# Products of rotated weights half a key step later, transposed results copied in halves, convolution rows loaded piece by piece

## The chip, the cores and the metric

The kernel runs on one core of a Trainium2 chip. The metric is the device time of one execution in microseconds (us), the median of the runs shown. In the profile, PE is TensorE (PEld its weight loads), DVE is VectorE, ACT is ScalarE, POOL is GpSimd, and SP is SyncE, whose queue issues all DMA transfers of this kernel.

## The reference, cut to what matters

Sixteen images of 256 channels and 64 x 64 pixels go through two layers, each of the form `x = x + f(groupnorm(x))`. Layer 0 is a grouped 3 x 3 convolution whose weights are rotated for each image by an angle that depends on the image. Layer 1 is linear attention with a 5 x 5 depthwise convolution of the values.

```python
# layer 0, f = rotated group convolution
pooled = x.mean(axis=(2, 3))
h = relu(pooled @ ap_w1.T + ap_b1)
angles = tanh(h @ ap_w2.T + ap_b2) * (pi / 4)
rot = vmap(vmap(_rotate_one))(base_kernel, angles)   # bilinear: 9 x 9 mixing of each 3 x 3 kernel
out = conv(x, rot, groups=B * G, padding=1)
feat = out * sigmoid(relu(pooled @ meta_w1.T + meta_b1) @ meta_w2.T + meta_b2)
# layer 1, f = focused linear attention
q = focus(relu(xt @ Wq.T + bq)); k = focus(relu(xt @ Wkv_k.T + bk)); v = xt @ Wkv_v.T + bv
z = 1 / (q . k.sum() + 1e-6)                          # focus: r -> r**3 * |r| / |r**3|
out = (q @ (k.T @ v)) * z + depthwise5x5(v) + dwc_b
out = out @ Wproj.T + bproj
```

All arithmetic is in float32.

## The kernel before

Everything is one hand-written order of instructions for each engine (`tc.manual_schedule()`, main loop from L930). An engine runs its instructions in the order in which the program emits them, so a place in this order is a place in every queue. The images overlap: while image b is in its attention, image b+1 is convolved, and image b+2's statistics are taken.

One image b of the main loop has three parts.

**Key steps** (`key_step`, L774). Sixteen steps n, of which images 1 to 15 do the first three already at the end of the previous image's attention, so that their loop starts at n = 3 (`LEAD`). Step n makes the keys and values of 256 pixels on PE (`key_products`, L559, two halves j), and adds bias and applies relu on DVE (`key_bias`: L528, L529, and L568 for the values). The focus function of a key block is spread over later steps: squares of block n-1 on ACT (L535), its cube on POOL (L538), then one step later the ratio on DVE (L543, L544), the root on POOL (L547) and the scaling on ACT (`key_scale`, L579). `values` (L592) multiplies scaled keys with values on PE into `pkv`: block 0 at step 3, then at each odd step blocks n-4 and n-3. `key_store` (L573, SP) writes the values to a DRAM image `vpad`, and `load_blocks` (L614, SP) reads them back as `vh`, the blocks of the depthwise convolution, two transfers a step from step 7 to step 14.

Beside the key steps runs the preparation of image b+1's rotated weights, a Python generator `prepare` (L190) called `made` in the loop. Each `next(made)` emits the instructions up to the next `yield`; `key_step` calls it twice a step, in the middle (after the first half's bias) and at the end. For image 0's key steps, `made` starts at step 1. For later images it starts with three advances in the attention steps p = 15, 16 and 17 of the image before, and goes on at step 3. The generator makes the angle terms, then for each half t of the channels and each n three kernel rows: `products` (L285, POOL, 128 x 864 elements), a pause, `reduce` (L301, DVE), a pause. After the third one `finish` adds row sums on DVE (L305) and the identity on POOL (L311). `spread` (L316, ACT) copies the result into the weight tile `wt`, and `shifts` (L324 to L328) makes the edge corrections in the last advance.

**Between** (`between`, L800). PE computes the first query block (L654), convolution unit 0 of image b+1 (L406, 288 products on 32 x 32 tiles), the remaining `values`, and the first half of the depthwise products `pd` (L629, 256 matmuls).

**Attention steps** (`attention_step`, L839), p = 1 to 17. Step p turns queries (`turn`, L669; copy `turned`, L674), multiplies them with the key-value state (`attend`, L686, result `o` on POOL, L697), turns the result of block p-2 back (`turn_back`, PE L705, copied from PSUM to the tile `oT` by ACT, L707) and projects it (`project`, L715). `project` has four products, two per half t of `oT`, in the order t = 0, 1, 0, 1. `add_up` (L727) and `store` (L733) finish block p-3; the store is one transfer for two blocks. Convolution units 1, 2 and 3 of image b+1 are emitted at the end of steps 3, 7 and 11 (`UNITS`), their evictions (L419) in the step after. The second depthwise half stands in step 9. Image b+2's statistics are loaded (L97) and taken (L106) in steps 3, 5, 7, 9 and 11 (`STATS`); there is one buffer for them, so a load waits on SP until DVE has taken the one before.

A convolution unit reads four pieces of rows, one per quarter q of the partitions (`xr`, one buffer for all images after image 0). `load_rows` (L376, SP) issues the four transfers of a unit together: unit 0 at key step 11, unit 1 in `between` ahead of the depthwise products, units 2 and 3 in attention steps 4 and 8, ahead of the stores. `load_edges` (L390, POOL) fills the rows beyond the image in the first and last pieces.

Of the kernel before, what the change touches and what calls it, by code (L numbers as in the profile page):

```python
# [15 lines left out]
P = 128  # L16
C = 256
H = W = 64
N = H * W
HID = 64  # L20
NH, HD = 8, 32
CH = 512
NCH = N // CH
# [5 lines left out]


UNITS, SECOND = {3: 1, 7: 2, 11: 3}, 9

STATS = {3: (0, 1), 5: (2,), 7: (3, 4), 9: (5, 6), 11: (7,)}
CROWS = CH + 2 * W
# [16 lines left out]
def conv_attention(ctx: ExitStack, tc: tile.TileContext, x, consts, kw, b1, w2, b2, b2r,  # L51
                   wkv, wq, brow, srow, wp, bp, dwb, band, out):
    nc = tc.nc
# [30 lines left out]
    state = {}  # L84
# [59 lines left out]
    def rows_of(b, u):  # L144
        return xbuf[u if b == 0 else 0]
# [44 lines left out]
    def prepare(b):  # L190

        a, pooled, mean = yield from gn_coefs(state[b]["st"], b, 0)
# [36 lines left out]
        edge = wtp.tile([P, NH], F32, tag="edge", name=f"edge_{b}")  # L229
# [2 lines left out]
        nc.vector.tensor_copy(edge, pe)  # L232
        state[b]["edge"] = edge
        if b == 0:
            load_edges(0, 0)
        nc.vector.tensor_scalar(mod, mod, 0.5, 0.5, ALU.mult, ALU.add)
        yield

# [93 lines left out]
        if b == 0:  # L332
            made = {k: products(*k) for k in ((0, 0), (0, 1), (0, 2), (1, 1), (1, 2))}
            made[1, 0] = own_products(1, 0)
            for t in range(2):
                for n in range(3):
                    reduce(t, n, made[t, n])
                row_sums(t)
                nc.vector.scalar_tensor_tensor(rots[t][:, 4], sel[:, 0:HD], 1.0, rots[t][:, 4], ALU.mult, ALU.add)
                if t == 0:  # L340
                    spread(0, range(4))
            for j in range(3):
                for q in (1, 3):
                    nc.vector.tensor_copy(wt[ts(q, HD), j], rots[1][ts(j, HD)])
            spread(1, (3,))
            state[b]["late"] = shifts
            return
        for t in range(2):
            for n in range(3):
                tmp = products(t, n)  # L350
                if t == 1 and n < 2:
                    spread(0, (2 * n,))
                yield
                reduce(t, n, tmp)
                if n == 2:
                    finish(t)
                yield
                if t == 1 and n < 2:
                    spread(0, (2 * n + 1,))
        for j in range(4):  # L360
            spread(1, (j,))
            yield
        for _ in range(3):
            yield
        shifts(0)
        shifts(1)

    def load_rows(b, u):


        for q in range(4):
            i, t = 2 * u + q // 2, q % 2
            lo, hi = max(0, CH * i - W), min(N, CH * (i + 1) + W)
            d = rows_of(b, u)[ts(q, HD)]
            at = W if i == 0 else 0
            nc.sync.dma_start(d[:, :, at:at + hi - lo], x[b, ts(t, P)].rearrange("(g c) n -> c g n", g=4)[:, :, lo:hi])  # L376

    def load_edges(b, u):


        for q in range(4):
            i, t = 2 * u + q // 2, q % 2
            mean = state[b]["edge"][ts(q, HD), ts(t, 4)].unsqueeze(2).to_broadcast([HD, 4, W])
            d = rows_of(b, u)[ts(q, HD)]
            for edge, at in ((0, 0), (NCH - 1, CROWS - W)):
                if i == edge:
                    if b == 0:
                        nc.scalar.copy(d[:, :, at:at + W], mean)
                    else:
                        nc.gpsimd.tensor_copy(d[:, :, at:at + W], mean)  # L390

    def convolve(b, u):

# [48 lines left out]
    nc.gpsimd.tensor_scalar(su, se, 1.0, None, ALU.add)  # L442
    nc.scalar.activation(sa, su, AF.Ln)
    for u in range(NCH // 2):
        load_rows(0, u)
    for i in range(2):
        load_stats(1, i)
    eps_t = const("eps", [P, C])
# [3 lines left out]
    for name, src, bsrc in (("kv", wkv, brow[C:3 * C]), ("q", wq, brow[0:C])):  # L452
        n = src.shape[1]
# [29 lines left out]
    for (w, br), lo in zip(wl.values(), (0, 2 * C)):  # L483
# [3 lines left out]
        n = w.shape[2]  # L487
# [82 lines left out]
    def key_store(b, n):  # L570
        for j in range(2):
            k, y = (2 * n + j) % BC, ROWS * (n // 2) + 2
            nc.sync.dma_start(vpad[b % 2][k, y:y + ROWS].rearrange("y j n -> (y j) n"),  # L573
                              vbuf[n % NV][:, j, 0:HD, :].rearrange("p c h -> p (c h)"))
# [125 lines left out]
    def turn_back(b, m):  # L700

        po = bank(f"po_{b}_{m}").rearrange("p (t j n) -> p t j n", t=2, j=2)
        for j in range(2):
            for t in range(2):
                nc.tensor.transpose(po[:, t, j, :], state[b]["o"][j][:, ts(t, P)], ident)  # L705
        oT = op.tile([P, 2, 2 * P], F32, tag="oT", name=f"oT_{b}_{m}", bufs=1)
        nc.scalar.copy(oT.rearrange("p t (j n) -> p t j n", j=2), po)  # L707
        state[b]["oT"] = oT

    def project(b, m):  # L710
# [29 lines left out]
    for u in range(NCH // 2):  # L740
        convolve(0, u)
        if u == 0:
            for t in range(2):
                state[0]["late"](t)
            load_edges(0, NCH // 2 - 1)
            for i in range(2, 6):
                load_stats(1, i)
        else:
            for i in {1: (0, 1), 2: (2, 3), 3: (4, 5)}[u]:
                take_stats(1, i)  # L750
                if u == 2:
                    load_stats(1, i + 4)
        for q in range(4):
            evict(0, u, q)
            settle(0, u, q)
# [44 lines left out]
    def between(b, more):  # L800

        k, f = state[b]["k"], state[b]["f"]
        query_products(b, 0)
        if more:
            convolve(b + 1, 0)
        ratio(k[NP - 2], False)
        root(k[NP - 2])
        squares(k[NP - 1], 0)
        cube(k[NP - 1])
        key_scale(b, NP - 2)  # L810
        query_bias(b, 0)
        blocked(b, 2)
        squares(k[NP - 1], 1)
        ratio(k[NP - 1], False)
        root(k[NP - 1])
        key_scale(b, NP - 1)
        squares(f[0], 0)
        cube(f[0])
        for n in range(NP - LATE, NP - 1):
            values(b, n)  # L820
        query_products(b, 1)
        query_bias(b, 1)
        values(b, NP - 1)
        if more:
            for q in range(4):
                evict(b + 1, 0, q)
        squares(f[0], 1)
        squares(f[1], 0)
        if more and b + 2 < B:
            load_stats(b + 2, 0)  # L830
        if more:
            load_rows(b + 1, 1)
        for c in range(0, HD, 4):
            depthwise(b, 0, c)
        if more:
            for q in range(4):
                settle(b + 1, 0, q)

    def attention_step(b, p, chain):  # L839
# [3 lines left out]
        more = b + 1 < B  # L843
# [69 lines left out]
        if p <= NCH:  # L913
            load_blocks(b, 2 * p + 14)
            load_blocks(b, 2 * p + 15)
        if u and u < 3:
            load_edges(b + 1, u + 1)
            load_rows(b + 1, u + 1)
        if p >= 3:
            store(b, p - 3)  # L920
        if n >= 1:
            key_store(b + 1, n - 1)
        if more and p in UNITS:
            u = UNITS[p]
            convolve(b + 1, u)
# [4 lines left out]
    with tc.manual_schedule():  # L930
        fold_load(0, "q")
        made = iter(())
        for b in range(B):
            more = b + 1 < B
            state[b]["f"], state[b]["xq"] = {}, {}
            for n in range(0 if b == 0 else LEAD, NP):
                if b == 0 and n == 0:
                    load_kernels(1)
                if b == 0 and n == 1:
                    made = prepare(1)  # L940
                key_step(b, n, made)
                if n >= 1:
                    key_store(b, n - 1)
                if b > 0 and n == LEAD:
                    fold_load(b, "q")
                if n == 5:
                    fold_scale(b, "q")
                if n == 6:
                    fold_shift(b, "q")
                if 7 <= n < 15:  # L950
                    load_blocks(b, 2 * n - 14)
                    load_blocks(b, 2 * n - 13)
                if more and n == 11:
                    load_edges(b + 1, 0)
                    load_rows(b + 1, 0)
                if NP - 3 <= n < NP - 1:
                    blocked(b, n - NP + 3)
            key_store(b, NP - 1)
            for _ in made:
                pass  # L960
            between(b, more)
            chain = None
            for p in range(1, NP + 2):
                if more and p == 12:
                    fold_load(b + 1, "kv")
                if more and p == 13:
                    chain = norm1(b + 1)
                    next(chain)
                if b + 2 < B and p == NP - 1:
                    made = prepare(b + 2)  # L970
                    load_kernels(b + 2)
                attention_step(b, p, chain if p >= 13 else None)
                if p >= NP - 1:
                    next(made, None)
            add_up(b, NP - 1)
            store(b, NP - 1)
            del state[b]
# [71 lines left out]
```

## Time and profile before

| | |
|---|---|
| median of three runs | 3645.0 us (3638.3 to 3660.34) |
| the profiled execution | 3636.04 us |
| its span, first to last instruction | 3634.3 us |
| mean granted TensorE clock | 0.990 |
| PE busy | 3475.8 us |
| DMA queue of the kernel | 507.26 MB |
| `xr` row transfers (L376) | 244 of 288 or 320 KB |
| `products` on POOL (L285) | 95, 1925 ns each |
| `reduce` on DVE (L301) | 96, 1052 ns each |
| `oT` copies on ACT (L707) | 256 of 128 x 512 elements, 586 ns each |
| edge copies on POOL (L390) | 60, 392 ns each |

A line of a timeline shows start and length in us, engine, line, operation, the tiles written and read, and how often it came; brackets hold the idle time of the engine ahead of it and what ended it. A line of waits shows who waited for whom, the total in us, how often, and the longest. SPq is SP's issuing of transfers. Each product leaves two matmul records (2,048 of L559 for 1,024 products).

### The profile page before, as it was taken

Reading aid. Unit: us, or ns where it says so; the run is one execution under the profiler, and the core shown is the slowest. Engines: PE = TensorE matmul, PEld = TensorE weight load, DVE = VectorE, ACT = ScalarE, POOL = GpSimd, SP = SyncE. Lnnn points to the kernel's source line nnn. Section 1 sums busy time; section 2 is a strip of 40 time slices with the busy share of each in tenths; the row PEclk is TensorE's granted clock in tenths of the full one; section 3 lists DMA queues with packets and bytes.
Section 4 is the critical chain, followed back from the end, with each engine's and each line's share of the span. In section 5 each row is a group of like instructions: output and inputs, shape, how many; then the busy total and the mean of one; then the engine's idle time right before and its main releaser. Section 6 shows DMA issues by size and latency. Waiting matters only on the chain. (4 is left out here: it accounts for less than half of the span.)

```text
span 3634.3 us, 114472 instructions
## 1 busy us (share of the span) xinstructions
PE 3475.8 (96%) x46568; PEld 2684.7 (74%) x46568; DVE 2289.3 (63%) x6541; ACT 2004.0 (55%) x6499; POOL 1619.8 (45%) x1803
## 2 busy tenths in 40 slices
PE   6999999999999999999999999999999999999999
PEld 3687786877768777687776867767677686876878
DVE  6766566665656756567565675656756566565656
ACT  2654646546465564645556455564555655556565
POOL 3534445444354543445435353443534545344445
PEclk9999999999999999999999999999999999999999
DMA  7462644536345363553535545255462554525342
GB/s 209 135 175 87 176 126 153 162 104 177 108 154 175 102 182 100 152 168 112 183 97 162 150 138 167 89 159 150 137 175 84 164 151 145 172 83 155 101 145 100
DMA packets 219857, 514.58 MB, mean 142 GB/s; under 512 B 26645, under 2 KB 99863, under 8 KB 207044
## 3 DMA queue, kind: packets, MB, share of 16 engines
q1 hardware_dynamic: 219332, 507.26, 45.4%
q8 instruction: 368, 6.03, 0.7%
q14 instruction: 157, 1.29, 0.1%
HBM read 371.63 MB, written 135.53 MB: 140 GB/s over the span
## 5 line engine op out<-in xcount | busy, mean ns | idle before, releaser
L559 PE MATMUL pk<-wkv,x 128*128 128x512 f32 x2048 | 972.9, 623 | 0.0
L697 POOL TENSOR_TENSOR o<-o,fm 128x256 f32<-128x256 f32 x512 | 362.1, 728 | 991.6 <-DVE o L695 870.2
L559 PEld LDWEIGHTS pk<-wkv,x 128*128 128x128 f32 x2048 | 617.8, 311 | 229.4 <-issue 30.7
L406 PE MATMUL pc<-xr,wt 32*32 32x504 f32 (+1 forms) x17568 | 607.4, 594 | 14.4 <-ACT wt L316 12.7
L406 PEld LDWEIGHTS pc<-xr,wt 32*32 32x32 f32 x17568 | 385.8, 103 | 201.4 <-issue 72.2
L715 PE MATMUL py<-oT,wp 128*128 128x256 f32 x2048 | 505.6, 390 | 0.9 <-ACT oT L707 0.7
L654 PE MATMUL pq<-wq,xq 128*128 128x256 f32 x2048 | 487.8, 381 | 0.0
L535 ACT ACTIVATE r_k<-rk 128x256 f32<-128x256 f32 x1024 | 415.1, 406 | 107.4 <-POOL rk L538 56.3
L535 ACT ACTIVATE r_q<-rq 128x256 f32<-128x256 f32 x1024 | 413.9, 408 | 81.7 <-DVE rq L529 52.4
L419 ACT ACTIVATE x<-pc,shift 128x512 f32<-128x512 f32 x256 | 165.5, 690 | 446.3 <-PE pc L406 425.0
L579 ACT ACTIVATE rk<-rk,s_k 128x256 f32<-128x256 f32 x512 | 231.7, 499 | 322.5 <-POOL s_k L547 322.5
L715 PEld LDWEIGHTS py<-oT,wp 128*128 128x128 f32 x2048 | 369.2, 189 | 51.6 <-issue 3.6
L654 PEld LDWEIGHTS pq<-wq,xq 128*128 128x128 f32 x2048 | 369.0, 190 | 41.9 <-ACT x L419 0.2
L528 DVE TENSOR_TENSOR pq<-pq,bq 128x512 f32<-128x512 f32 x256 | 177.5, 693 | 317.8 <-PE pq L654 317.8
L707 ACT COPY oT<-po 128x512 f32<-128x512 f32 x256 | 150.0, 586 | 392.7 <-PE po L705 392.1
L547 POOL TENSOR_TENSOR s_k<-s_k,phalf 128x2 f32<-128x2 f32 x256 | 176.9, 691 | 425.3 <-DVE s_k L544 419.2
L538 POOL TENSOR_TENSOR rk<-r_k,rk 128x512 f32<-128x512 f32 x256 | 327.1, 1278 | 57.2 <-ACT r_k L535 54.9
L538 POOL TENSOR_TENSOR rq<-r_q,rq 128x512 f32<-128x512 f32 x256 | 326.6, 1276 | 29.9 <-issue 29.9
L547 POOL TENSOR_TENSOR s_q<-s_q,phalf 128x2 f32<-128x2 f32 x256 | 179.1, 700 | 347.4 <-DVE s_q L544 318.2
L528 DVE TENSOR_TENSOR pk<-pk,bkv 128x256 f32<-128x256 f32 x512 | 218.5, 427 | 132.6 <-PE pk L559 131.7
L686 PE MATMUL pn<-kvx,qT 128*128 128x132 f32 x2048 | 273.3, 276 | 0.0
L629 PE MATMUL pd<-vh,band 107*32 107x128 f32 x8192 | 243.8, 277 | 22.9 <-issue 22.6
(135 smaller groups left out, 5012.4 us busy)
## 6 DMA issues: line engine op xcount, KB each, us to landing
vh<-vpad SPq DMA_DIRECT2D x256, 384.0 KB
vh<-vpad SPq DMA_DIRECT2D x256, 360.0 KB
vpad<-v SPq DMA_DIRECT2D x512, 128.0 KB
out<-x SPq DMA_DIRECT2D x128, 512.0 KB
xr<-in_x SPq DMA_DIRECT2D x182, 320.0 KB
xs<-in_x SPq DMA_DIRECT2D x224, 256.0 KB
xr<-in_x SPq DMA_DIRECT2D x62, 288.0 KB
xs<-in_x SPq DMA_DIRECT2D x16, 512.0 KB
```

The costliest lines, as they stand in the source:

```text
L406: nc.tensor.matmul(pcs[q].rearrange("p (r w) -> p r w", w=W)[ts(j, HD), :, to:to + n], lhsT=wt[ts(q, HD), j, k, :], rhs=g[ts(q, HD), j, r: ...
L528: nc.vector.tensor_add(pm, pm, bias)
L535: nc.scalar.activation(f["r2"][:, j, :], f["r"][:, j, :], AF.Square, accum_out=f["s"][:, k, j:j + 1])
L538: nc.gpsimd.tensor_mul(f["r"], f["r2"], f["r"])
L547: nc.gpsimd.tensor_tensor(f["s"][:, 3, :], f["s"][:, 2, :], phalf, ALU.pow)
L559: nc.tensor.matmul(pm, lhsT=state[b]["x"][n // 2][:, t, T % BC:CH:BC], rhs=w[:, t, :], start=t == 0, stop=t == 1)
L579: nc.scalar.mul(f["r"][:, j, :], f["r"][:, j, :], f["s"][:, 3, j:j + 1])
L629: nc.tensor.matmul(pd[ts(j, HD), k, :].rearrange("p (R m h) -> p R m h", R=4, m=4), lhsT=band_t[:, c + k, :], rhs=vb[:, :, :, j, c + k, :] ...
L654: nc.tensor.matmul(pq[:, j, :], lhsT=xq[:, t, ts(j, P)], rhs=w[:, t, :], start=t == 0, stop=t == 1)
L686: nc.tensor.matmul(pn[:, :, 4 * hh:4 * hh + 4], lhsT=qT[:, hh, j, :], rhs=kvx[:, hh], start=True, stop=True)
L697: nc.gpsimd.tensor_add(o, o, fm[:, 2 * (m % NCH) + j, :])
L715: nc.tensor.matmul(py[:, co].rearrange("p y (J c) -> p J y c", c=BC), lhsT=wp_t[:, t, ts(co, P)], rhs=oT[:, t, :].rearrange("p (J y c) -> ...
```

## The change

Three things are changed; what is computed stays the same.

1. `prepare` has one more pause ahead of the products and one less at its end. The advances before the products and the one with `shifts` stay where they are; products, sums, finishing adds and spreading move by half a key step.
2. `turn_back` copies `po` to `oT` in two instructions, one per half t, where there was one.
3. `load_rows` and `load_edges` are cut into one piece per call (`load_edge`, `load_rows` with q). Unit 0's pieces are emitted one a step at key steps 11 to 14. Units 1, 2 and 3 follow the table `PIECES` in the attention steps 1 and 2, 4 to 6, and 8 to 10, behind the step's store and key store and ahead of its convolution. Nothing is left of row loads in `between`. The first image's loads in the prologue keep their order.

```diff
+PIECES = {1: ((1, 0), (1, 1)), 2: ((1, 2), (1, 3)), 4: ((2, 0),), 5: ((2, 1), (2, 2)), 6: ((2, 3),),
+          8: ((3, 0),), 9: ((3, 1), (3, 2)), 10: ((3, 3),)}
...
             state[b]["late"] = shifts
             return
+        yield
         for t in range(2):
             for n in range(3):
                 tmp = products(t, n)
...
-        for _ in range(3):
+        for _ in range(2):
             yield
         shifts(0)
...
-    def load_rows(b, u):
-        for q in range(4):
-            i, t = 2 * u + q // 2, q % 2
-            lo, hi = max(0, CH * i - W), min(N, CH * (i + 1) + W)
-            d = rows_of(b, u)[ts(q, HD)]
-            at = W if i == 0 else 0
-            nc.sync.dma_start(d[:, :, at:at + hi - lo], x[b, ts(t, P)].rearrange("(g c) n -> c g n", g=4)[:, :, lo:hi])
+    def load_rows(b, u, q):
+        i, t = 2 * u + q // 2, q % 2
+        lo, hi = max(0, CH * i - W), min(N, CH * (i + 1) + W)
+        at = W if i == 0 else 0
+        nc.sync.dma_start(rows_of(b, u)[ts(q, HD), :, at:at + hi - lo],
+                          x[b, ts(t, P)].rearrange("(g c) n -> c g n", g=4)[:, :, lo:hi])
...
+    def load_edge(b, u, q):
+        i, t = 2 * u + q // 2, q % 2
+        if i not in (0, NCH - 1):
+            return
+        at = CROWS - W if i else 0
+        to = rows_of(b, u)[ts(q, HD), :, at:at + W]
+        mean = state[b]["edge"][ts(q, HD), ts(t, 4)].unsqueeze(2).to_broadcast([HD, 4, W])
+        if b == 0:
+            nc.scalar.copy(to, mean)
+        else:
+            nc.gpsimd.tensor_copy(to, mean)
...
         oT = op.tile([P, 2, 2 * P], F32, tag="oT", name=f"oT_{b}_{m}", bufs=1)
-        nc.scalar.copy(oT.rearrange("p t (j n) -> p t j n", j=2), po)
+        for t in range(2):
+            nc.scalar.copy(oT[:, t, :].rearrange("p (j n) -> p j n", j=2), po[:, t])
...
         if more and b + 2 < B:
             load_stats(b + 2, 0)
-        if more:
-            load_rows(b + 1, 1)
         for c in range(0, HD, 4):
             depthwise(b, 0, c)
...
-        if u and u < 3:
-            load_edges(b + 1, u + 1)
-            load_rows(b + 1, u + 1)
         if p >= 3:
             store(b, p - 3)
         if n >= 1:
             key_store(b + 1, n - 1)
+        for u, q in PIECES.get(p, ()) if more else ():
+            load_edge(b + 1, u, q)
+            load_rows(b + 1, u, q)
         if more and p in UNITS:
...
-                if more and n == 11:
-                    load_edges(b + 1, 0)
-                    load_rows(b + 1, 0)
+                if more and 11 <= n < 15:
+                    load_edge(b + 1, 0, n - 11)
+                    load_rows(b + 1, 0, n - 11)
```

More of the change, by code (lines that the diff above doesn't have):

```diff
@@ L234, in prepare @@
         if b == 0:
-            load_edges(0, 0)
+            for q in range(2):
+                load_edge(0, 0, q)
         nc.vector.tensor_scalar(mod, mod, 0.5, 0.5, ALU.mult, ALU.add)
@@ L366, in prepare @@
         shifts(1)
-    def load_rows(b, u):
-        for q in range(4):
-            i, t = 2 * u + q // 2, q % 2
-            lo, hi = max(0, CH * i - W), min(N, CH * (i + 1) + W)
-            d = rows_of(b, u)[ts(q, HD)]
-            at = W if i == 0 else 0
-            nc.sync.dma_start(d[:, :, at:at + hi - lo], x[b, ts(t, P)].rearrange("(g c) n -> c g n", g=4)[:, :, lo:hi])
[L378 to L390, printed above, removed]
+    def load_rows(b, u, q):
[15 more added lines that the diff above has]
+            nc.gpsimd.tensor_copy(to, mean)
     def convolve(b, u):
@@ L444, in conv_attention @@
     for u in range(NCH // 2):
-        load_rows(0, u)
+        for q in range(4):
+            load_rows(0, u, q)
     for i in range(2):
@@ L744, in conv_attention @@
                 state[0]["late"](t)
-            load_edges(0, NCH // 2 - 1)
+            for q in range(2, 4):
+                load_edge(0, NCH // 2 - 1, q)
             for i in range(2, 6):
```

## The prediction

> **What bounds the kernel now.** I read the page first, then TensorE's own waits, then busy time by stretch, then the timeline of single steps.
>
> ```profile
> PE 3475.8 (96%) x46568; PEld 2684.7 (74%) x46568; DVE 2289.3 (63%) x6541; ACT 2004.0 (55%) x6499; POOL 1619.8 (45%) x1803
> ```
>
> TensorE is the bound, and the change takes no matrix product away. What can be won is its idle time, 3634.3 - 3475.8 = 158.5 us, and what hides inside "busy". Its longest waits:
>
> ```profile
> PE pkv L592 <- ACT rk L579: 65.3, 37, 3.2
> PE pd L629 <- issue: 22.6, 19, 2.1
> ```
>
> The first is the key-value products waiting for scaled keys, in the key steps of images 1 to 14. Image 0 has the same products and hardly waits. Two stretches with the same work, from the first key product of step 6 to the next image's convolution unit 0, in images 0 and 7 (length, then busy time by engine, clock, DMA share):
>
> ```profile
> 125.69:171.40 45.71, 45.71 (x466) 32.30 (x460) 38.98 (x105) 36.43 (x129) 33.25 (x31) 1.00 0.69 211
> 1688.93:1741.27 52.34, 47.18 (x466) 32.55 (x461) 35.01 (x101) 32.97 (x118) 31.52 (x31) 0.97 0.59 190
> ```
>
> Both have 466 matmuls. Image 7 idles 5.16 us, and its clock is 0.97: in 1728.40 to 1731.90 the granted clock was 0.51, right after the wait of 3.2 us, and 16 key products took 8.59 us there instead of 7.26. Why it waits shows in one key step of image 7:
>
> ```profile
> 1716.28 0.84 PE L592 MATMUL pkv<-v,rk 128*32 128x33 f32 x32 [1.96 <-ACT rk L579]
> ...
> 1716.89 1.91 POOL L285 TENSOR_TENSOR rtmp<-mix,kw 128x864 f32<-128x864 f32 x1
> ...
> 1718.83 1.05 DVE L301 TENSOR_REDUCE rot<-rtmp 128x96 f32<-128x864 f32 x1 [1.66 <-POOL rtmp L285]
> ...
> 1720.23 0.69 POOL L547 TENSOR_TENSOR s_k<-s_k,phalf 128x2 f32<-128x2 f32 x1 [1.43 <-DVE s_k L544]
> ```
>
> GpSimd makes a product in the middle of the step, VectorE sums it at the end, and the next step's ratio (L543, L544) stands behind that sum on VectorE, so the next root waits for the product. Root 0.65, cube 1.24, product 1.91, sum 1.05 and ratio 0.4 make a ring of 5.24 us a step (roots at 1714.99 and 1720.23). TensorE needs (7.26 + 1.20) / 2 = 4.23. In image 0 the generator started at another half step, so products lie at the end of a step and sums in the middle of the next:
>
> ```profile
> 134.78 1.04 DVE L301 TENSOR_REDUCE rot<-rtmp 128x96 f32<-128x864 f32 x1
> ...
> 135.71 1.92 POOL L285 TENSOR_TENSOR rtmp<-mix,kw 128x864 f32<-128x864 f32 x1
> ...
> 137.72 0.69 POOL L547 TENSOR_TENSOR s_k<-s_k,phalf 128x2 f32<-128x2 f32 x1
> ```
>
> The ratio no longer waits for the sum: roots come at 133.81 and 137.72, 3.91 us apart, under TensorE's 4.23. The second wait lies in the depthwise products, while four row transfers run (1751.5 to 1758.5: DMA share 0.92):
>
> ```profile
> 1757.94 5.29 PE L629 MATMUL pd<-vh,band 107*32 107x128 f32 x185 [0.77 <-issue]
> ```
>
> **Part 1, the pause.** It moves images 1 to 14 into the arrangement that image 0 shows. GpSimd's order stays root, cube, product; only the sum's place on VectorE moves. Queued behind the moved sum are the second half's bias and relu; they have slack, since VectorE's step is 2.60 + 1.05 = 3.65. Steps with the finishing add are longer in image 0 too (roots 137.72 to 142.58: 4.86), and no wait follows. The stretch lasted 52.09 to 52.62 in images 1 to 14, mean 52.28: 14 x (52.28 - 45.71) = -92.0. Image 0 gets the pause as well; its products then fall in the middle of step 6, as images 1 to 14 have it now: +6.6. Its scale in step 6 comes 4.9 us after that step's first key product, theirs 4.8, so it should lose the same. Together -85.4; bounds 0 (the wait moves) and -92.0 (image 0 keeps its slack).
>
> **Part 2, rows leave the stretch of the depthwise products.** From unit 0's convolution to the end of the first depthwise half takes 21.57 to 25.10 us, mean 23.06. Its waits (22.6 us over the run) follow late instruction fetches: a packet of 16 KB on the instruction queue at 1755.20 took 1.34 us, at 1530.88 1.37, and TensorE stood at 1757.18 and 1531.73. Image 15 loads no rows and its depthwise half took 7.20 without a wait. So -22; three of these waits are followed by 3.4 us at half clock, -4; and the convolution itself started 0.5 late in images 1 to 14, its bank held by the late bias steps (13.75 to the depthwise start against 13.17 in image 0), -7. Sum -33, bounds 0 and -38.
> The Trainium skill speaks against it: "Runtime: NRT & Kernel Launch", Instruction fetch mechanics, has TensorE's instructions prefetched in blocks of 16 KiB into room for 2048 and calls the fetch hidden. By that rule the -26 of the waits would not come, and the sum would be 3553 instead of 3527; the row above, a wait after each slow fetch, is what I follow.
>
> **Part 3, what the pieces cost.** The number of transfers stays. Each issue is 0.33 to 0.49 us on SP, and SP is no bound. They move behind other things in its queue. Row transfers take 1.6 us each with all engines busy (1751 to 1759: 80% of 8 us for four), block loads 1.05 (1763.2 to 1778.1: 42.3% of 14.9 us for six).
> Unit 0: three of four move behind up to six key stores and six block loads, to step 14. From step 11 to the last piece there is some 16 us of DMA work (1717 to 1742: 70.6% of 25 us, less the stores behind it) in the 20 us before the convolution. The last lands 2.5 us early to 1 us late: 0.4 x 15 = +6.
> Unit 1: now behind four block loads that wait for the depthwise end (1763.27). 4 x 1.05 + 4 x 1.6 = 10.6 us at full share, 12 to 14 at the shares seen, and the convolution starts 14.75 us later: 0.2 x 15 = +3.
> Unit 2: the last piece stands at step 6 behind this:
>
> ```profile
> 1799.48 1.00 SPq L97 DMA_DIRECT2D xs<-in_x  x2
> 1800.54 1.59 SPq L614 DMA_DIRECT2D vh<-vpad  x2
> 1802.23 0.44 SPq L733 DMA_DIRECT2D out<-x  x1
> ```
>
> SP is held until 1799.48 by the statistics. The store's packets end 0.1 to 0.9 us before the convolution at 1809.07 in images 1 to 14, and a row transfer adds 1 to 1.8: 0.8 x 14 = +11. Unit 3's last piece goes out about 1838 for 1847.41: nothing. Sum +20, bounds 0 and 44 x 1.5 = 66.
> The edge copies on GpSimd (0.39 each) go one per step, behind one root and cube; the middle of a step has that slack. If the cover were gone: 4 x 15 x 0.39 = 23.
>
> **Part 4, halves.** One copy of 512 elements becomes two of 256. SBUF copies of 256 took 406 ns (L646); PSUM's were not seen, so 293 (half of 586) to 586.
>
> ```profile
> 1801.18 0.59 ACT L707 COPY oT<-po 128x512 f32<-128x512 f32 x1 [1.43 <-PE po L705]
> ...
> 1801.83 1.99 PE L715 MATMUL py<-oT,wp 128*128 128x256 f32 x8
> ```
>
> The first weight load waits for it, 0.06 after its end, in nearly every step: 1801.816 instead of 1801.717, and the second matmul comes 0.311 after the first instead of 0.216. That is 0.095 a step. A first half of 406 ends at 1801.59 and removes it: 240 x 0.095 = -23; I take -20, since the second half (to 1801.99) is needed by the third matmul at 1802.04. ScalarE's extra 0.2 a step lies in its 1.4 us idle before that copy. Dependence by slices is seen at 1716.28: a product starts before the second of two scalings ends. If it waited for both, +0.13 to +0.22 a step, +31 to +54.
>
> **Sum.** 3636.0 (the profiled run, span 3634.3) - 85.4 - 33 + 20 - 20 = 3517.6. The median of the runs, 3645.0, lies 9.0 above it; with that, 3527.
>
> **Rivals.**
> A: the late pieces hold the convolutions, and it ends slower. For: units 0 and 2 land within a microsecond of need. Against: DMA share falls to 0.04 before unit 1. From waits near 1.9 us the clock halves, as at 1716.30 (1.96 idle) and 1728.40, for 1.33 more. 44 waits (units 0 and 1 in 15 images, 2 in 14) eat the 138 us won from 1.8 us each; at 2.5 each, 44 x 3.83 = 169 and 3675.
> The Trainium skill, "TensorE: Matmul & The Clock Gate", Part 1, lets the clock fall only after about 3.4 us idle; then 44 x 2.5 = 110 and 3617. The stretches above show it sooner, so I keep 1.33.
> B: the key chain still holds TensorE, since sums now delay the second half's relu: part 1 gives nothing, 3645 - 33 = 3612. Against it stands image 0.
> C: the depthwise waits stay, or move to other dense products, so 26 are not won: 3527 + 26 = 3553. For: the DMA work is the same in sum. Against: image 15.
> D: the projection waits for both halves: 3527 + 20 + 43 = 3590.
>
> **How the numbers follow.** Forecast 0.61, C 0.13, D 0.10, B 0.09, A 0.07. The likeliest alone reaches from 3490 (no row waits, no offset of 9) to 3560. The range goes on to D's 3600 and leaves out A and B, 0.16. A measurement tells about 1% from no change: below 3608.6 lie forecast, C and D, 0.84; B is within 1%, 0.09; A above, 0.07.
>
> **What would show it.** Waits of L592 on L579 only in image 0, about 5 us; key roots 3.9 us apart in images 1 to 14; the stretch of 52.3 near 46. No wait in the first depthwise half. The wait of the second `py` matmul gone. Small waits of the convolutions for `xr` transfers, at unit 2 above all. I am wrong if these are near 2 us each, or if L592 goes on waiting.

## The result, and the profile after

The changed kernel takes 3670.16 us (median of 20 runs, 3648.81 to 3689.89) against 3649.18 for the kernel before (20 runs, 3638.3 to 3660.34). The ratio is 1.0059, with a 95% interval of 1.0043 to 1.0076: 0.6% slower, where 3.2% faster was forecast. The profiled execution took 3662.93 us, its span is 3661.0 us, and the mean granted clock is 0.979.

The first lines to hold against those of before are the busy times of the page, then TensorE's waits (who waited for whom, total in us, how often, longest), both of the changed kernel. Its line numbers are a few higher: L410 is the convolution (L406 before), L564 the keys, L597 the key-value products, L634 the depthwise products, L721 the projection. Counts of products in these lines are records, two for each product, so a convolution unit's x288 stands for 144 products.

```profile
PE 3488.0 (95%) x46568; PEld 2656.3 (73%) x46568; DVE 2321.8 (63%) x6541; ACT 2021.7 (55%) x6755; POOL 1623.5 (44%) x1803
```

```profile
PE pc L410 <- DMA xr<-in_x: 90.3, 55, 4.2
...
PE pkv L597 <- ACT rk L584: 4.3, 3, 2.6
```

The wait that the change was aimed at fell from 65.3 us to 4.3, and the depthwise waits (22.6 us before) are no longer in the list. In their place, one group that did not exist stands on top: convolutions that wait for rows, 90.3 us. But idle time grew only by 14.5 us (3661.0 - 3488.0 = 173.0, was 158.5). Busy time grew too, by 12.2, with the same instructions: in these two traces TensorE was granted half clock for 72.9 us before and for 153.6 after. So a list of waits does not show the whole price here. The lengths of the stretches do. These are sums over the run, from the start and end times of the products in the traces; "early" and "best" are two versions of the experiments below.

| us, summed over the images | before | after | early | best |
|---|---|---|---|---|
| key step 6 to unit 0, image 0 | 45.7 | 51.7 | 50.2 | 45.7 |
| key step 6 to unit 0, images 1 to 14 | 732.0 | 632.5 | 632.8 | 632.8 |
| convolution unit 0, 15 images | 153.8 | 214.5 | 147.9 | 146.4 |
| unit 1 | 145.0 | 218.0 | 148.6 | 149.7 |
| unit 2 | 145.4 | 184.3 | 157.2 | 154.6 |
| unit 3 | 148.8 | 147.5 | 154.4 | 149.0 |
| first depthwise half, 15 images | 140.0 | 108.0 | 108.0 | 108.0 |
| second depthwise half, 15 images | 112.3 | 108.0 | 112.4 | 110.0 |
| all the rest | 2011.3 | 1996.5 | 1998.0 | 1994.4 |
| span | 3634.3 | 3661.0 | 3509.5 | 3490.6 |

Every gain came: 93.5 us in the key steps, 32.0 + 4.3 in the depthwise halves, 14.8 in the rest. Units 0, 1 and 2 lost 60.7 + 73.0 + 38.9 = 172.6, and that is the whole result.

The gains in the changed kernel's own lines. First the same stretch as before in images 0 and 7 (length, busy time by engine, clock, DMA share, GB/s):

```profile
127.52:179.27 51.75, 47.86 (x467) 32.47 (x461) 35.06 (x101) 34.88 (x122) 32.79 (x31) 0.97 0.63 195
1706.27:1751.44 45.17, 45.17 (x465) 32.39 (x460) 38.60 (x105) 33.91 (x119) 32.53 (x31) 1.00 0.69 213
```

Image 7 took 52.34 before and now has no idle time at all; image 0 has taken the wait over. In a key step of image 7 GpSimd's product comes 1.9 us after the root, the sum stands in the middle of the step, and the roots (L552) are 3.92 us apart:

```profile
1714.28 0.69 POOL L552 TENSOR_TENSOR s_k<-s_k,phalf 128x2 f32<-128x2 f32 x1
...
1715.32 1.04 DVE L305 TENSOR_REDUCE rot<-rtmp 128x96 f32<-128x864 f32 x1
...
1716.17 1.93 POOL L289 TENSOR_TENSOR rtmp<-mix,kw 128x864 f32<-128x864 f32 x1
...
1718.20 0.69 POOL L552 TENSOR_TENSOR s_k<-s_k,phalf 128x2 f32<-128x2 f32 x1
```

The first depthwise half of the same image runs in one piece, and the page's groups for projection and copies (busy us, mean ns; 505.6 us of L715 and 586 ns before) show the halves:

```profile
1769.66 7.20 PE L634 MATMUL pd<-vh,band 107*32 107x128 f32 x256
```

```profile
L721 PE MATMUL py<-oT,wp 128*128 128x256 f32 x2048 | 484.0, 379 | 0.5 <-ACT oT L713 0.5
...
L713 ACT COPY oT<-po 128x256 f32<-128x256 f32 x512 | 165.6, 375 | 390.5 <-PE po L710 390.0
```

Now the loss. SP's issues and TensorE's products around unit 1 of image 8, the convolution that runs during image 7's attention:

```profile
1776.91 1.59 SPq L619 DMA_DIRECT2D vh<-vpad  x2
1778.60 0.92 SPq L379 DMA_DIRECT2D xr<-in_x  x2
1779.58 1.60 SPq L619 DMA_DIRECT2D vh<-vpad  x2
1781.22 1.39 SPq L379 DMA_DIRECT2D xr<-in_x  x2
1782.65 2.58 SPq L619 DMA_DIRECT2D vh<-vpad  x2
```

```profile
1791.51 1.09 PE L410 MATMUL pc<-xr,wt 32*32 32x512 f32 x16
1794.49 1.93 PE L410 MATMUL pc<-xr,wt 32*32 32x512 f32 x8 [1.89 <-DMA xr<-in_x]
1796.67 10.91 PE L410 MATMUL pc<-xr,wt 32*32 32x512 f32 x264 [0.24 <-DMA xr<-in_x]
```

The last piece was issued 9 us before the convolution began and still was not there. After waits of 1.89 and 0.24 us the remaining 264 records took 10.91 us. The reason is in the clock of the same stretch, cut into four (length, PE busy, clock, DMA share, GB/s):

```profile
1791.92:1795.33 3.41, 1.52 (x21) 0.87 0.98 225
1795.34:1798.75 3.41, 3.17 (x50) 0.50 0.51 141
1798.76:1802.10 3.34, 3.34 (x79) 0.63 0.19 59
1802.20:1805.60 3.40, 3.40 (x124) 1.00 0.94 277
```

TensorE is nearly always busy from 1795.34 on, yet gets through 50 and 79 records where it later does 124. A wait of 2.13 us has cost this unit 16.07 - 9.67 = 6.40 us (9.67 is an undisturbed unit). Units 0 and 2 look the same:

```profile
1751.44 1.19 PE L410 MATMUL pc<-xr,wt 32*32 32x512 f32 x24
1755.84 10.23 PE L410 MATMUL pc<-xr,wt 32*32 32x512 f32 x264 [3.21 <-DMA xr<-in_x]
...
1828.67 1.19 PE L410 MATMUL pc<-xr,wt 32*32 32x512 f32 x24
1832.40 10.04 PE L410 MATMUL pc<-xr,wt 32*32 32x512 f32 x264 [2.55 <-DMA xr<-in_x]
```

### The profile page after: what moved, and what is told of

It is laid out like the page before. It is cut to its first block, busy times and chain, and to the rows that moved or that the text cites. A ratio compares the mean times of both kernels' runs of the same rounds, so it can differ in the third digit from the quotient of the medians.

```text
span 3661.0 us, 114794 instructions
## 1 busy us (share of the span) xinstructions
PE 3488.0 (95%) x46568; PEld 2656.3 (73%) x46568; DVE 2321.8 (63%) x6541; ACT 2021.7 (55%) x6755; POOL 1623.5 (44%) x1803
## 5 line engine op out<-in xcount | busy, mean ns | idle before, releaser
L564 PE MATMUL pk<-wkv,x 128*128 128x512 f32 x2048 | 951.1, 611 | 0.0
L410 PE MATMUL pc<-xr,wt 32*32 32x504 f32 (+1 forms) x17568 | 683.6, 646 | 109.8 <-DMA xr<-in_x 90.3
L564 PEld LDWEIGHTS pk<-wkv,x 128*128 128x128 f32 x2048 | 616.4, 311 | 208.9 <-issue 2.8
L410 PEld LDWEIGHTS pc<-xr,wt 32*32 32x32 f32 x17568 | 382.1, 107 | 376.7 <-issue 240.4
L721 PE MATMUL py<-oT,wp 128*128 128x256 f32 x2048 | 484.0, 379 | 0.5 <-ACT oT L713 0.5
L552 POOL TENSOR_TENSOR s_q<-s_q,phalf 128x2 f32<-128x2 f32 x256 | 179.3, 700 | 535.6 <-DVE s_q L549 406.0
L721 PEld LDWEIGHTS py<-oT,wp 128*128 128x128 f32 x2048 | 370.4, 190 | 45.9 <-issue 3.6
L713 ACT COPY oT<-po 128x256 f32<-128x256 f32 x512 | 165.6, 375 | 390.5 <-PE po L710 390.0
L584 ACT ACTIVATE rk<-rk,s_k 128x256 f32<-128x256 f32 x512 | 231.6, 499 | 194.5 <-POOL s_k L552 192.9
L552 POOL TENSOR_TENSOR s_k<-s_k,phalf 128x2 f32<-128x2 f32 x256 | 177.2, 692 | 337.4 <-DVE s_k L549 323.3
L109 DVE BATCH_NORM_STATS2 st<-xs 128x6 f32<-128x512 f32 x256 | 165.8, 685 | 233.6 <-DMA xs<-in_x 233.0
```

Of the source, the lines that this page charges most:

```text
L410: nc.tensor.matmul(pcs[q].rearrange("p (r w) -> p r w", w=W)[ts(j, HD), :, to:to + n], lhsT=wt[ts(q, HD), j, k, :], rhs=g[ts(q, HD), j, r: ...
L552: nc.gpsimd.tensor_tensor(f["s"][:, 3, :], f["s"][:, 2, :], phalf, ALU.pow)
L564: nc.tensor.matmul(pm, lhsT=state[b]["x"][n // 2][:, t, T % BC:CH:BC], rhs=w[:, t, :], start=t == 0, stop=t == 1)
L584: nc.scalar.mul(f["r"][:, j, :], f["r"][:, j, :], f["s"][:, 3, j:j + 1])
L721: nc.tensor.matmul(py[:, co].rearrange("p y (J c) -> p J y c", c=BC), lhsT=wp_t[:, t, ts(co, P)], rhs=oT[:, t, :].rearrange("p (J y c) -> ...
```

## The experiments

**1 and 2: the change taken apart.** One kernel has the pause and the halves, with rows loaded as before; the other has only the rows in pieces.

```diff
 # e1: the kernel before, with
+        yield
...
-        for _ in range(3):
+        for _ in range(2):
...
-        nc.scalar.copy(oT.rearrange("p t (j n) -> p t j n", j=2), po)
+        for t in range(2):
+            nc.scalar.copy(oT[:, t, :].rearrange("p (j n) -> p j n", j=2), po[:, t])
 # e2: the kernel before, with load_edge, load_rows(b, u, q) and PIECES of the change
```

> Half step and halved copies, row loads as they were before. Theory Q (the pause and the halves give what was forecast, and the changed kernel loses it because pieces of rows stand too late in the transfer queue): in the changed kernel the stretch from key step 6 to the convolution lasted 45.2 us instead of 52.3 (14 images, -99), image 0 lost 6, the projection gained some 23; so 3649 - 116 = about 3533, with the waits of the first depthwise half still there (20 to 27 us) and each of the convolution units 0 to 2 at about 9.7 us. Rival S (TensorE reaches the convolutions so much earlier that rows are late wherever they are loaded): unit 0 waits here as well, and the time stays above 3600.

> The kernel before with the pieces alone. Theory Q: units 1 and 2 wait as in the changed kernel (4.9 and 2.6 us a unit, 15 images: +112); unit 0 hardly waits, since the key steps are slower here; the waits of the first depthwise half go (-26): about 3735. Rival S: the pieces do no harm at the old pace of TensorE, only the 26 us go: about 3620.

Without the pieces it took 3544.87 us against 3650.38, ratio 0.9716 (0.9691 to 0.9740); that is 12 us more than expected, with depthwise waits of 32.9 us where 20 to 27 were expected. With the pieces alone it took 3723.75, ratio 1.0221 (1.0184 to 1.0257). TensorE's waits, first of the kernel without pieces, then of the one with nothing else:

```profile
PE pd L630 <- issue: 32.9, 25, 3.2
...
PE pkv L593 <- ACT rk L580: 4.8, 3, 3.2
```

```profile
PE pkv L596 <- ACT rk L583: 63.7, 38, 2.6
PE pc L409 <- DMA xr<-in_x: 58.3, 44, 3.7
```

The loss belongs to the pieces, and the gain of the key steps to the pause. The two kernels do not add up to the change, though: -105.5 and +73.4 make -32, and the change is +21. In the traces units 0, 1 and 2 lose 25.8 + 61.4 + 33.4 = 120.6 us with the pieces alone and 172.6 with all parts. Unit 0 was expected hardly to wait with the pieces alone, and it lost 25.8 us; with all parts it lost 60.7. The stretch ahead of it took 51.8 us on average in the first case and 45.2 in the second (images 1 to 14). Image 0 has it the other way round, and its numbers turn round too: with the pieces alone its stretch took 45.69 us and the unit behind it 13.84, with all parts 51.75 and 9.67. So for unit 0 the pause makes the time shorter in which the pieces must land. For units 1 and 2 (17.1 of the 52 us) no run separates the pause from the halves.

**3 and 4: the same pieces, earlier.** Only the table and, in the second, the key steps of unit 0 change.

```diff
 # e3: the changed kernel, with
-PIECES = {1: ((1, 0), (1, 1)), 2: ((1, 2), (1, 3)), 4: ((2, 0),), 5: ((2, 1), (2, 2)), 6: ((2, 3),),
+PIECES = {1: ((1, 0), (1, 1), (1, 2), (1, 3)), 4: ((2, 0),), 5: ((2, 1), (2, 2)), 6: ((2, 3),),
 # e4 ("early"): the changed kernel, with
+PIECES = {1: ((1, 0), (1, 1), (1, 2), (1, 3)), 4: ((2, 0), (2, 1)), 5: ((2, 2), (2, 3)),
...
-                if more and 11 <= n < 15:
+                if more and 5 <= n < 9:
```

> The changed kernel with all four pieces of unit 1 in attention step 1, so behind two block loads instead of four; units 0 and 2 unchanged. Theory Q (place in the queue decides): unit 1 goes from 14.5 us to about 9.7, 15 times: 3670 - 73 = 3597. Rival K (row transfers are slow beside block loads wherever they stand, since all share the same engines): unit 1 stays at 13 to 14.5 us, 3650 to 3670.

> The changed kernel with pieces moved forward: unit 0 at key steps 5 to 8, unit 1 in attention step 1, unit 2 in steps 4 and 5, two each. Theory Q: all three units at about 9.7 us, which takes 15 x (4.6 + 4.9 + 2.6) = 181 us off: about 3489. Rival K: units go on waiting, above 3600.

Unit 1's last two pieces one step earlier: 3602.62 us, ratio 0.9872 (0.9853 to 0.9892). Unit 1's mean length fell from 14.53 to 10.14 us, units 0 and 2 stayed (14.03 and 12.79). All pieces early: 3511.70, ratio 0.9620 (0.9601 to 0.9639), with the waits that are left on the convolutions, and unit 1 of image 8, where the changed kernel waited 1.89 us:

```profile
PE pc L410 <- issue: 13.2, 11, 1.9
...
PE pc L410 <- DMA xr<-in_x: 1.9, 2, 1.2
```

```profile
1712.60 9.67 PE L410 MATMUL pc<-xr,wt 32*32 32x512 f32 x288
```

So neither the cut nor the number of transfers loses this time. The place in SP's order at which the late pieces are issued does. The 23 us by which the second run missed its 3489 stand mostly under units 1 to 3 in the table (4, 12 and 9 us above the 145 of 15 undisturbed units): in units 2 and 3 small waits on the instruction stream, 11.7 of the 13.2 us above, and what follows them.

**5 and 6: pause alone, halves alone.** Each is its two or three lines of the diff on the kernel before.

> The kernel before with the pause moved, and nothing else. By the stretches of the run without pieces (45.2 us for 14 images, 52.4 for image 0, against 52.3 and 45.7): 3650 - 93 = 3557, waits of L592 on the scaling in image 0 alone. Rival: part of what the run without pieces won came only with the halves, since the two act in different parts of an image they should add; then more than 3575.

> The kernel before with oT copied in halves, and nothing else. If the projection waits for slices: the attention of eight steps ahead of the second depthwise half goes from 63.07 to 62.46 us as in the run without pieces, 16 images and the steps behind it likewise: 3650 - 19 = 3631. Rival D (waits for both halves): slower, 3680 to 3700.

The pause alone: 3559.10 against 3652.51, ratio 0.9745 (0.9724 to 0.9766). The halves alone: 3634.53, ratio 0.9957 (0.9938 to 0.9975). Both came within 4 us of what was expected. Rival D, a projection that waits for both halves, falls. The traced execution of the halves alone was the slowest of its six (3663.21); its projection was busy for 484.0 us, as in the changed kernel.

**7: unit 1's rows out of the depthwise stretch, nothing else.** The whole unit moves to attention step 1 in the kernel before.

```diff
-        if more:
-            load_rows(b + 1, 1)
         for c in range(0, HD, 4):
             depthwise(b, 0, c)
...
+        if more and p == 1:
+            load_rows(b + 1, 1)
```

> The kernel before with only unit 1's four row transfers moved from ahead of the first depthwise half to attention step 1, behind two block loads. Theory F (the transfers hold up the fetch of TensorE's instructions there): the waits of the first depthwise half (22 us, and some 4 of half clock) go and nothing comes back, unit 1 at 9.7 to 10.2 us: 3650 - 24 = 3626. Rival: the waits are of another cause, or move to the next dense products (unit 1): 3645 to 3655.

3635.14 against 3652.51, ratio 0.9954 (0.9934 to 0.9974). The first depthwise half took 7.20 us in every image, as in the changed kernel. What is left of the waits on the instruction stream, in its trace:

```profile
PE pd L629 <- issue: 11.9, 8, 4.1
...
PE pc L406 <- issue: 6.0, 9, 1.9
```

The first line is the second depthwise half (112.3 us before, 129.3 here); units 1 to 3 took 5 us more each. So 32.0 us went from the first half, but the median fell by 17, to a place between what theory F (3626) and its rival (3645 to 3655) expected. By the packet records, 1,035 row packets of unit 3 ran beside the second half in this trace and 303 in the trace of before, so more rows met depthwise products there. How much of this a usual execution pays is open: the traced one (3639.06 us) was the slowest of six, and that of before (3636.04) was faster than all nine beside it.

**8 and 9: other transfers beside the depthwise products.** The version of experiment 4, first with four copies from `x` to a spare DRAM tile ahead of the first depthwise half, then with unit 1's own rows issued there as well as at step 1.

```diff
         # e9, e11: in between, ahead of the depthwise products
+        if more:
+            for q in range(4):
+                nc.sync.dma_start(spare[q], x[b + 1, ts(q % 2, P), 0:CROWS])   # e9
+                load_rows(b + 1, 1, q)                                          # e11
         for c in range(0, HD, 4):
             depthwise(b, 0, c)
```

> The version with early pieces (3512), with four additional copies of 320 KB from the input to unused DRAM, placed where unit 1's row loads stood before, ahead of the first depthwise half. Nothing waits for them, and the output does not depend on them. Theory F: any transfers there hold up the fetch, so the depthwise waits come back, 20 to 33 us: 3535 to 3545. Rival: the waits came from the row loads themselves or from what waits for them: depthwise half stays at 7.2 us, 3512 to 3518.

> The version with early pieces, and unit 1's four row transfers issued twice: once ahead of the first depthwise half as in the kernel before, where they wait for the end of convolution unit 0 and so run during the depthwise products, and again at attention step 1. The first set is overwritten by the second, so what is added is 1.3 MB of transfers at that place (this was meant with the spare copies, which waited for nothing and ran 5 us too early, from 1682 to 1689 us, and were over before the depthwise half at 1694.7). Theory F, transfers beside the depthwise half hold up its instruction fetch: the waits of about 1.5 to 2.2 us per image come back in that half, 22 to 33 us, 3534 to 3545 us. Rival, the waits came from where the fetch stood in the order and not from transfers: 3510 to 3514.

The spare copies gave 3509.67, ratio 0.9616 (0.9594 to 0.9637): no wait came back, against the expectation. Its windows (length, busy time by engine, clock, DMA share, GB/s) show that the test had missed its place. In 1682 to 1689, during the convolution, the copies ran; in the depthwise half the DMA engines stood almost still:

```profile
1682.00:1689.00 7.00, 7.00 (x218) 4.73 (x208) 1.96 (x6) 4.89 (x19) 2.88 (x4) 1.00 0.88 270
1694.67:1701.87 7.20, 7.20 (x266) 7.00 (x258) 4.74 (x14) 4.73 (x11) 1.94 (x2) 1.00 0.02 5
```

Rows have to wait for unit 0 to release `xr`; the copies waited for nothing. With the rows issued twice, 3540.11 us, ratio 0.9711 (0.9695 to 0.9728), 0.9% or some 33 us above experiment 4, as theory F expected. The first depthwise half took 144.3 us over the run instead of 108.0. Its waits, and image 7:

```profile
PE pd L634 <- issue: 22.5, 16, 3.1
```

```profile
1702.27 2.13 PE L634 MATMUL pd<-vh,band 107*32 107x128 f32 x67
1707.53 6.98 PE L634 MATMUL pd<-vh,band 107*32 107x128 f32 x189 [3.13 <-issue]
```

Row transfers beside the depthwise products bring the waits, wherever else the rows are loaded. The packets on the instruction queue show how. In experiment 4 a packet of 16 KB started 1.3 to 3.1 us ahead of the first depthwise product in all 15 images; in image 7 at 2.21 us ahead, the next one 2.21 us after it, of 1.39 and 1.29 us, and there was no wait. With the rows issued twice, none started in image 7 between 5.42 us ahead and 2.57 us after; that one took 1.37 us, and TensorE stood from 2.13 to 5.26 us. The packet is late, not slow.

In the run with the spare copies, unit 0 had no wait at the DMA share of 0.88 (10.04 us on average, 9.86 in experiment 4). That holds for these copies, which go to DRAM, and not for convolutions at large: units 1 to 3 of the same run had nine waits on the instruction stream, 6.2 us in all, the longest 1.54 in unit 2 of image 8 at a DMA share of 0.59.

**10 and 11: a better version.** The early pieces, with image 0's generator left as it was; and the same with units 2 and 3 loaded whole.

```diff
 # e8 ("best"): experiment 4, with
-        yield
+        if b > 1:
+            yield
...
-        for _ in range(2):
+        for _ in range(2 if b > 1 else 3):
 # e10: the same, with
+PIECES = {1: ((1, 0), (1, 1), (1, 2), (1, 3)), 4: ((2, 0), (2, 1), (2, 2), (2, 3)),
+          8: ((3, 0), (3, 1), (3, 2), (3, 3))}
```

> The version with early pieces, with the new pause only from the third image's weights on: the weights that are made beside image 0's key steps keep the half step they had. Image 0's stretch from key step 6 to convolution unit 0 took 50.2 and 51.9 us with the pause in the two runs of early pieces and 45.7 in the kernel before. If the pause does there what it did in the other fifteen intervals, the other way round, 4 to 6 us go: 3506 to 3508 us, ratio about 0.961. Rival: 3512 as without this edit, if the next wait in image 0 takes the place of the one removed.

> As the run beside it (early pieces, image 0 without the pause), but units 2 and 3 are loaded whole, four transfers at attention steps 4 and 8, so that nothing is left of loading piece by piece except for unit 0. Theory: the cut itself costs nothing and brings nothing, only the time of the last piece counts; then the same time within 4 us, 3504 to 3511. Rival: four transfers together hold up block loads and stores enough for a new wait; 3515 or more. The other rival: the small waits left in units 2 and 3 (11.7 us over the run of early pieces) come from pieces that are still late, and go; 3496.

3495.30 us against 3647.82, ratio 0.9594 (0.9569 to 0.9619), and 3506.04, ratio 0.9623 (0.9594 to 0.9652). Image 0's stretch is 45.70 us again. The first came out 11 us below its expectation. The second hit its own, but lies 10.7 us above the first, where the two were expected within 4. The intervals overlap, so the medians do not tell whether loading piece by piece is worth anything. The traces show a price in one place: with units loaded whole, 2,601 row packets ran beside the second depthwise halves, which took 121.7 us; with pieces 84, and 110.0. Unit 2 took 5.7 us less in exchange. The first is the fastest kernel of this study, 4.1% below the kernel before:

```profile
PE 3409.3 (98%) x46568; PEld 2660.4 (76%) x46568; DVE 2329.2 (67%) x6541; ACT 2019.5 (58%) x6755; POOL 1622.3 (46%) x1803
```

## Why the prediction was wrong, point by point

**The bound** was right: TensorE's idle time, and what hides in "busy". The second half of that sentence is where the loss went.

**Part 1 (-85.4)** was right. Images 1 to 14 gained 99.5 us, image 0 lost 6.0, together -93.5. The stretch became 45.18 on average, a little less than the 45.71 that image 0 had lent as the measure. The pause alone gave 93 us at the median.

**Part 2 (-33)** came out in size, partly by luck: the first depthwise half gave -32.0 where -26 was set, and the -7 for a convolution that started late does not show in the changed kernel, whose unit 0 waits for rows (it shows where the rows are there in time: unit 0 -5.9 with early pieces, -4.5 with the pause alone). Its mechanism was argued from slow packets on the instruction queue, of 1.34 and 1.37 us. Their length is not the cause: experiment 4 has one of 1.39 in a half without a wait. Experiment 11 shows that the row transfers are the cause, and that the packet starts late. "Runtime: NRT & Kernel Launch" of the Trainium skill, section Instruction fetch mechanics, calls the crossing of a 16 KiB block mostly hidden. In this case it is not: 15 depthwise halves took 36.3 us longer with row transfers beside them (144.3 against 108.0), and had no wait without. What the prediction left out is the second half, where waits come with rows of unit 3 (experiments 7 and 10); the changed kernel has no rows there, and that half gave another 4.3 us.

**Part 4 (-20)** was right: `py` busy time fell by 21.6 us, the second matmul came 0.216 us after the first (median; 0.311 before), and the halves alone gave 18 at the median. A first half of 375 ns was inside the bounds.

**Part 3 (+20, bounds 0 and 66) is the step that failed.** Units 0, 1 and 2 measured +60.7, +73.0 and +38.9, where +6, +3 and +11 were set. Three things were wrong with it.

First, the landing. The prediction added prices that transfers have alone, for what SP issues ahead of the last piece: 10.6 us for unit 1, "12 to 14 at the shares seen", within 14.75. In image 8 the last row packet ended at 1795.06, 18.2 us after the depthwise end (packet records of the trace); in all 15 images it was 16.3 to 19.5 us, and the convolution came 14.65 us after it. The first packet of the first block load started only 1.55 us after its issue (1776.91). The two block loads issued behind the pieces were served among them: 131 of the 144 block packets of the six loads, so at least 35 of the 48 behind, had started before the last row packet did. And packets were longer in this mix: 1,091 ns for 16 KB of a block load, 694 when block loads ran alone before; 205 against 198 ns for a row. Six block loads and four rows make 2.2 + 6.5 + 6.6 = 15.3 us of 16 engines. And the end of the packets is not the end of the wait: the waiting product started a median of 1.2 us after the last row packet had ended (41 waits of units 0 to 2; 0.6 to 1.8 in all but one). Neither this nor the 1.55 us at the start stands in the prediction's sum. For unit 2 the single piece was issued 6 us before the convolution (1822.61), with four block loads and a store around it; its packets ran from 1824.94 to 1830.89, where 1.6 us had been its price. How much of this the loads behind the pieces cause and how much the late issue, no run separates: in experiment 3 both improve at once (in image 8, 64 of the 144 block packets started before the last row packet, which ended 2.9 us before the convolution).

Second, the parts were costed apart. The 20 us ahead of unit 0 in which its pieces were to land are those of the kernel before; the pause takes time out of them. In the changed kernel unit 0's last row packet ended 1.3 to 6.2 us after the convolution's first product in images 1 to 14, where 2.5 us early to 1 us late was set. Between experiment 2 and the whole change the units lose 52 us more (120.6 and 172.6), 34.9 of them in unit 0.

Third, the price of a wait. The waits themselves sum to 96.4 us in the 45 units, 2.14 each; the units lost 181.6 us against 45 undisturbed ones of 9.67, 4.04 each. The 140 us at half clock in them account for up to 70 of the remaining 85. Part 3 counted microseconds of lateness only.

**The rivals.** A was the case that came, and its arithmetic was good: waits of 1.8 us each as the break-even, 1.33 for the clock on top, 3675 at 2.5 each. Measured: 2.14 and 1.9, and 3670. It was given 0.07 because "DMA share falls to 0.04 before unit 1". That share was of the kernel before, whose rows were already there; the change fills that very gap. B and D are refuted by experiments 5 and 6. C is refuted for the changed kernel, whose two depthwise halves have no wait; in experiment 7 the second half keeps such waits, beside rows of unit 3. Taking part 3 away from the forecast gives 3507; the early pieces gave 3512, and 3495 with image 0 mended.

**What would show it.** The signs came as written: L597 waits for L584 three times, 3.9 of the 4.3 us in image 0, the roots are 3.92 us apart, the first depthwise half has no wait, and the convolutions wait for `xr` near 2 us each, which was the sign for being wrong.

**The clock.** The prediction kept 1.33 us for each wait from the stretches, against "TensorE: Matmul & The Clock Gate" of the Trainium skill, Part 1. The runs bear out that the clock halves after shorter waits: 26 of the 45 units 0 to 2 ran in part at half clock, and only four of them had a wait over 3.4 us. They also show it to be uneven: 1.89 us of waiting was followed by 6.83 us at half clock, while a wait of 2.82 us in unit 0 of image 11 was followed by none. The page's free-running window of 3.4 us fits the lengths found, 3.41 and 6.83; its condition of a whole idle window does not.

## What to carry to other kernels

A transfer that moves closer to its user must be costed in the queue that it will meet, with what is issued behind it too and with packets as long as they are in that mix, not by its own price alone; and in the time that is left after the other parts of the change have shortened it. Units that waited 2.14 us on average lost 4.04 here, so look at the lengths of stretches and not at the list of waits. Try the same pieces earlier before the idea is given up: here six key steps for unit 0 and one attention step for the late pieces of units 1 and 2 turned 0.6% slower into 3.8% faster.

## What the runs showed of the hardware that was not expected

- Row transfers beside the depthwise products delay TensorE's instructions: 15 halves took 36.3 us more (experiment 11), and had no wait without the transfers. The second half took 108.0 us in the three runs without a row packet beside it (the changed kernel, experiments 2 and 3) and 121.7 with 2,601 of them (experiment 10).
- What decides whether a transfer does this is open. The depthwise half leaves 266 matmul records and 258 weight loads in 7.20 us, 73 a microsecond, a unit 576 in 9.67, 60; but units 2 and 3 had such waits too (11.7 us in experiment 4), while unit 0 had none beside copies to DRAM at a DMA share of 0.88 (experiment 9).
- A copy of 256 elements from PSUM took 375 ns on ScalarE, one of 512 took 586.
- 16 KB packets of block loads took 694 ns alone and 1,091 among row transfers, and a product that waited for rows started 1.2 us (median) after their last packet had ended.
- Half clock after a wait of 1.89 us, full clock after one of 2.82.
